# Extra products of ones with bias rows behind the last transposes of each graph-convolution layer, and one shift copy used twice

## The chip, the cores and the metric

The kernel is one launch on one core of a Trainium2 chip. The number that counts is the device time of that launch in microseconds (us); three runs of the kernel before took 3001.92 to 3007.29 us, with a median of 3004.92 us. The core has five engines that run side by side and meet through semaphores: TensorE (PE in the profile: matrix products into PSUM, with its weight loads shown as PEld), VectorE (DVE), ScalarE (ACT), GpSimd (POOL) and SyncE (SP), whose queue here only issues transfers (SPq). The profile also lists the clock that TensorE was granted, as a share of full speed; in this case it is either 1.0 or 0.5 at any moment.

## The reference

Sixteen graphs of 1024 nodes with 128 features pass through four residual layers, each followed by a normalisation over features. The change touches the second of them, three rounds of graph convolution with a batch normalisation after each:

```
def _sage(x, adj, Wr, Wx, b, mf):
    deg = jnp.clip(jnp.sum(adj, axis=-1, keepdims=True), 1.0, None)
    agg = jnp.einsum('bij,bjd->bid', adj, x) / deg
    out = agg @ Wr + x @ Wx + b
    nrm = jnp.maximum(jnp.linalg.norm(out, axis=-1, keepdims=True), NORM_EPS)
    return out / nrm * mf[..., None]

def _bn(x, g, b):
    m = jnp.mean(x, axis=(0, 1)); v = jnp.var(x, axis=(0, 1))
    return (x - m) * jax.lax.rsqrt(v + BN_EPS) * g + b

h1 = _bn(relu(_sage(x, adj_d, Wr1, Wx1, b1, mf)), g1, be1)
h2 = _bn(relu(_sage(h1, adj_d, Wr2, Wx2, b2, mf)), g2, be2)
h3 = _bn(relu(_sage(h2, adj_d, Wr3, Wx3, b3, mf)), g3, be3)
out = concatenate([h1, h2, h3], -1) @ Wl + bl
```

The mean and variance run over all graphs and nodes, so no round can use its normalised input before the round ahead of it has been finished for every graph. `adj_d` keeps few edges; nearly all nodes have only the term `x @ Wx + b`. The biases `b1`, `b2`, `b3` are all zeros in these inputs.

## The kernel before, in words

The whole is a row of phases: attention over the sixteen graphs (`phase_att`), the search for the edges that survive (`phase_pattern`), the three convolution rounds (`phase_conv`, the place of the change), and the two last layers (`phase_end`). By the timeline `phase_conv` starts its products at 1956.8 us of the span and `phase_end` its own at 2294.8 us.

`phase_conv` runs `for layer in (1, 2, 3)` and inside it a software pipeline over `SETS` = 20 sets: 16 graphs and 4 sets of "slots" (the few nodes with edges), mixed by `ORDER`. At step `i` of `range(SETS + 3)` the program writes, in this order:

- `turn(layer, i - 3)`: eight PE transposes of `u` in two halves (L1487, into `pt`), DVE statistics of each half (L1491), ACT copies of each half (L1494), and for a graph a store of the result by SP (L1501);
- `norm(i - 1)` and `scale(i - 2)`: the row norm on DVE and POOL (L1460, L1462, L1463, L1465) and `u`, the scaled relu, on DVE (L1472);
- `start(layer, i + 3)`: the load of a later input (L1370);
- `product(layer, i)`: eight fp32 products (L1417; each stands in the profile as two records, so "x16"), for slots also L1430; then `values` for a slot set (L1401), and `add_bias` (L1438): two products of `all_ones` with a bf16 row block `rows`, 128x512 each; then `squares` on ACT (L1450, L1452).

The last three steps, i = 20, 21 and 22, have no product: they hold `turn(17)`, `turn(18)` and `turn(19)`, what is left of `norm` and `scale`, and the first loads of the next layer. Then a chain of small operations makes the normalisation's factor and shift (L1547 to L1567, one of them on POOL) in `bn`. The next layer folds them in: ACT scales the weights (`w_u`, L1511), and `shifted` makes a copy of the shift over a whole tile (`shift`, L1324), multiplies it by the weights (L1326) and adds the result to the bias (L1327); `spread` turns that into bf16 rows (L1309 to L1318). At step 1, behind the first bias products, `rescale(layer - 1)` folds the same factor and shift into the last linear map: a scaled copy of `wl` (L1332), then `shifted` once more with its own copy of the same `shift`. After layer 3 `rescale(3)` does it a last time, and `extra(b0, (2,))`, eight times, adds products for the slots (L1343, L1348), whose results POOL scatters (L1581) before `phase_end` loads x (L1606) and h (L1610) by SP.

Every engine keeps the program's order: at the end of `phase_conv` and of `phase_end` the instructions of each engine are tied to each other as written (`as_traced`). Three PSUM buffers `pq` (`ps_q`, two banks each) hold products, two buffers `pt` (`ps_t`) hold transposes and small products; a buffer is used again in turn.

The lines that put the change in its place:

```
            if i < SETS:
                product(layer, i, w_u)
                ...
                for k in ((), (0, 1))[i] if i < 2 else (i,):
                    add_bias(k, bias_u if ORDER[k] < B else ROWS[layer])
                    squares(k)
            elif layer < 3:
                start(layer + 1, i - SETS)
            if layer > 1 and i == 1:
                rescale(layer - 1)
```

Of the kernel before, what the change touches and what calls it, by code (L numbers as in the profile page):

```python
# [10 lines left out]
F32 = mybir.dt.float32  # L11
# [11 lines left out]
B, N, F = 16, 1024, 128  # L23
P = 128
T = N // P
# [1246 lines left out]
def phase_conv(ctx, tc, t, c, x1_d, x1T_d, slots_d, keep, uT_d):  # L1272
# [5 lines left out]
    nc = tc.nc  # L1278
# [3 lines left out]
    ps_q = ctx.enter_context(tc.tile_pool(name="b_pq", bufs=3, space=PSUM))  # L1282
# [3 lines left out]
    SETS = B + 4  # L1286
# [8 lines left out]
    wl = cp.tile([P, 3, F], F32, name="wl")  # L1295
# [3 lines left out]
    all_ones = cp.tile([P, P], BF16, name="all_ones")  # L1299
    nc.vector.memset(all_ones, 1.0)  # L1300

    def spread(row, name):

        rest = wp.tile([P, F], F32, name="rest", bufs=1)
        sums = wp.tile([P, F], F32, name="sums", bufs=1)
        part = wp.tile([P, F], BF16, name="part", bufs=1)
        for k in range(3):
            src = row if k == 0 else rest
            nc.vector.tensor_copy(part, src)  # L1309
            nc.vector.tensor_tensor(rest, src, part, ALU.subtract)  # L1310
            if k == 0:
                nc.vector.tensor_scalar(sums, part, c.ident[:, 0:1], None, op0=ALU.mult)
            else:
                nc.vector.scalar_tensor_tensor(
                    sums, part, c.ident[:, k : k + 1], sums, op0=ALU.mult, op1=ALU.add
                )
        rows = wp.tile([P, 4, F], BF16, name=name, bufs=1)
        nc.vector.tensor_copy(rows, sums.unsqueeze(1).to_broadcast([P, 4, F]))  # L1318
        return rows.rearrange("p a f -> p (a f)")

    def shifted(to, bn, w, name):

        shift = wp.tile([P, P], F32, name="shift", bufs=1)
        nc.vector.tensor_copy(shift, bn[:, 1:2].to_broadcast([P, P]))  # L1324
        pt = ps_t.tile([P, 4, P], F32, name="pt")
        nc.tensor.matmul(pt[:, 0, :], shift, w, start=True, stop=True)  # L1326
        nc.vector.tensor_tensor(to, to, pt[:, 0, :], ALU.add)  # L1327

    def rescale(layer):

        l, bn = layer - 1, keep.bn[layer - 1]
        nc.vector.tensor_scalar(keep.wl[:, l, :], wl[:, l, :], bn[:, 0:1], None, op0=ALU.mult)  # L1332
        shifted(keep.bl, bn, wl[:, l, :], "l")

    W2, BIAS, GB = {}, {}, {}

# [22 lines left out]
    ROWS = {layer: spread(BIAS[layer], f"rows{layer}") for layer in (1, 2, 3)}  # L1359
    H, Q, R, S, U, VALUES = {}, {}, {}, {}, {}, {}  # L1360

    def slots_at(s, l):
        return uS[:, l, (s - B) * N : (s - B + 1) * N]

    def start(layer, i):

        s = ORDER[i]
        hT = H[layer, i] = wp.tile([P, N], F32, name="hT", bufs=4)
        if s < B:
            nc.sync.dma_start(hT, x1T_d[s] if layer == 1 else uT_d[layer - 2][s])  # L1370
        return hT
# [62 lines left out]
    def add_bias(i, rows):  # L1434

        pq = Q[i]
        for half in range(2):
            nc.tensor.matmul(  # L1438
                pq[:, half * 4 : half * 4 + 4, :].rearrange("p t f -> p (t f)"), all_ones,
                rows, start=False, stop=True, skip_group_check=True,  # L1440
            )
# [13 lines left out]
    def norm(i):  # L1455

        s = ORDER[i]
        square, sq = S.pop(i)
        if i % 2 == 0:
            nc.vector.tensor_reduce(sq, square, AX.X, ALU.add)  # L1460
        nrm = R[i] = small.tile([P, T], F32, name="nrm")
        nc.gpsimd.tensor_scalar(sq, sq, NORM_EPS * NORM_EPS, None, op0=ALU.max)  # L1462
        nc.gpsimd.tensor_tensor(nrm, sq, c.mhalf, ALU.pow)  # L1463
        counts = valid[:, (s - B) * HALF : (s - B + 1) * HALF] if s >= B else keep.plain[:, s, :]
        nc.gpsimd.tensor_tensor(nrm, nrm, counts, ALU.mult)  # L1465

    def scale(i):
        u = U[i] = wp.tile([P, T, F], F32, name="u", bufs=3)
        pq, nrm = Q.pop(i), R.pop(i)
        n = T if i < SETS - 1 else T // 2  # L1470
        for k in range(0, T, n):
            nc.vector.scalar_tensor_tensor(  # L1472
                u[:, k : k + n, :], pq[:, k : k + n, :], 0.0, nrm[:, k : k + n].unsqueeze(2).to_broadcast([P, n, F]),
                op0=ALU.max, op1=ALU.mult,
            )

    def turn(layer, i):
        s, u = ORDER[i], U.pop(i)
        if s >= B:
            to = slots_at(s, layer - 1)  # L1480
        else:
            to = wp.tile([P, N], F32, name="uT")
        flat = []
        for half in range(2):
            pt = ps_t.tile([P, 4, P], F32, name="pt")
            for j in range(4):
                nc.tensor.transpose(pt[:, j, :], u[:, half * 4 + j, :], c.ident)  # L1487
            flat.append(pt.rearrange("p t i -> p (t i)"))

        def stats_of(half):  # L1490
            nc.vector.bn_stats(stats[:, 2 * s + half, :], flat[half])  # L1491

        def copy(half):
            nc.scalar.copy(to[:, half * 512 : half * 512 + 512], flat[half])  # L1494

        stats_of(0)
        stats_of(1)
        copy(0)
        copy(1)
        if s < B:  # L1500
            nc.sync.dma_start(uT_d[layer - 1][s], to)  # L1501
# [4 lines left out]
    for layer in (1, 2, 3):  # L1506
        bn = keep.bn[layer - 2]
        w, w_u, bias_u = W2[layer], W2[layer][:, :F], ROWS[layer]
        if layer > 1:
            w_u = wp.tile([P, F], F32, name="w_u", bufs=1)  # L1510
            nc.scalar.activation(w_u, w[:, :F], AF.Copy, scale=bn[:, 0:1])  # L1511
            bias_u = wp.tile([P, F], F32, name="bias_u", bufs=1)
            nc.vector.tensor_copy(bias_u, BIAS[layer])
            shifted(bias_u, bn, w[:, :F], "w")
            bias_u = spread(bias_u, "rows_u")
        assert ORDER[0] < B and ORDER[1] < B
        for i in range(SETS + 3):
            if i >= 3:
                turn(layer, i - 3)
            if 2 <= i <= SETS:  # L1520
                norm(i - 1)
            if 2 <= i < SETS + 2:
                scale(i - 2)
            if i + 3 < SETS:
                start(layer, i + 3)
            if layer == 3 and i == 3:
                nc.sync.dma_start(keep.adj, t["adjT"][0].rearrange("(t p) i -> p t i", p=P))
            if i < SETS:
                product(layer, i, w_u)
                if i + 1 < SETS:  # L1530
                    values(layer, i + 1)
                if i + 2 < SETS:
                    start_slots(layer, i + 2)
# [3 lines that stand above are left out]
                if i == 1:  # L1537
                    norm(0)
            elif layer < 3:
                start(layer + 1, i - SETS)  # L1540
            if layer > 1 and i == 1:
                rescale(layer - 1)
            if layer == 3 and 4 <= i < 4 + HALF:
                extra(2 * (i - 4), (0, 1))

        mv = small.tile([P, 2], F32, name="mv")
        nc.vector.bn_aggr(mv, stats.rearrange("p a b -> p (a b)"))  # L1547
        gb = GB[layer]
        more = SETS / B
        mean = small.tile([P, 2], F32, name="mean")  # L1550

        nc.vector.tensor_scalar(mean[:, 0:1], mv[:, 0:1], more, None, op0=ALU.mult)
        nc.vector.scalar_tensor_tensor(
            mean[:, 1:2], mv[:, 0:1], mv[:, 0:1], mv[:, 1:2], op0=ALU.mult, op1=ALU.add
        )
        sc = small.tile([P, 2], F32, name="sc")
        nc.vector.tensor_scalar(
            sc[:, 0:1], mean[:, 0:1], mean[:, 0:1], BN_EPS, op0=ALU.mult, op1=ALU.subtract
        )
        nc.vector.scalar_tensor_tensor(  # L1560
            sc[:, 0:1], mean[:, 1:2], more, sc[:, 0:1], op0=ALU.mult, op1=ALU.subtract
        )
        nc.gpsimd.tensor_tensor(sc[:, 1:2], sc[:, 0:1], c.mhalf[:, 0:1], ALU.pow)
        bn = keep.bn[layer - 1]
        nc.vector.tensor_tensor(bn[:, 0:1], sc[:, 1:2], gb[:, 0:1], ALU.mult)
        nc.vector.tensor_tensor(sc[:, 0:1], mean[:, 0:1], bn[:, 0:1], ALU.mult)
        nc.vector.tensor_tensor(bn[:, 1:2], gb[:, 1:2], sc[:, 0:1], ALU.subtract)  # L1567
    rescale(3)
    as_traced(tc, first)

# [973 lines left out]
```

## Time and profile before

| | |
|---|---|
| median of three runs | 3004.92 us |
| the profiled execution, its own time | 2989.07 us |
| its span, first to last instruction | 2987.1 us |
| mean granted TensorE clock | 0.947 |

The span in parts, with busy time of each engine, the granted clock (PEclk) and the share of the transfer engines. The rows are: layer 1 of the convolution, layer 2, layer 3, the passage to `phase_end`, and `phase_end`.

```profile
1956.50:2058.00 101.50, 86.18 (x680) 77.23 (x680) 63.52 (x83) 64.76 (x240) 42.57 (x61) 0.94 0.49 168
2058.00:2160.70 102.70, 85.17 (x652) 76.15 (x652) 66.50 (x95) 65.18 (x236) 42.57 (x61) 0.92 0.47 164
2160.70:2277.80 117.10, 99.09 (x780) 90.19 (x780) 71.95 (x103) 65.07 (x234) 42.55 (x61) 0.94 0.47 171
2277.80:2294.70 16.90, 10.79 (x66) 10.51 (x66) 5.82 (x11) 0.00 (x0) 9.00 (x9) 0.70 0.35 112
2294.70:2987.00 692.30, 645.58 (x5634) 635.18 (x5634) 469.64 (x1829) 265.67 (x576) 204.85 (x232) 0.98 0.42 152
```

The columns after the length are PE, PEld, DVE, ACT and POOL in us, then clock, transfers and GB/s. In the three layers PE is the busiest engine, at 83 to 85 us of each 100, and its clock is below full there.

### The profile page before, as it was taken

To read this page: it belongs to the slowest core of one execution; us is meant where nothing else is said; L and a number is where in the kernel's file an instruction comes from. 1 tells how busy PE (TensorE), PEld (TensorE's weight loads), DVE (VectorE), ACT (ScalarE), POOL (GpSimd) and SP (SyncE) were. 2 spreads that over 40 slices of the span, in tenths; PEclk is the share of its full clock that TensorE was granted. 3 is DMA by queue.
4 is the path that set the end of the run, shared out by engine and by line. 5 is a ranking of instruction groups with operands and counts; after the bars stand their busy time and mean duration, and the time that the engine had idled before them with its cause. 6 is when DMAs were issued, how large, how long until landed. Compare 5 with 4: busy or idle time off the path is not lost. (4 is left out here: it accounts for less than half of the span.)

```text
span 2987.1 us, 71058 instructions
## 1 busy us (share of the span) xinstructions
PE 2680.9 (90%) x25724; PEld 2405.8 (81%) x25724; DVE 2252.3 (75%) x8656; ACT 1841.4 (62%) x5689; POOL 1260.1 (42%) x1305
## 2 busy tenths in 40 slices
PE   5999999999999999999997898577896999999997
PEld 3888888888888888888887887367786999999996
DVE  5798888988898888988884568756655677677674
ACT  3888888788887888888883233255653433443333
POOL 3655455644555554654322433244433233333321
PEclk8999999999999999999997777788997999999999
DMA  5324332333224332332214542054555254445540
GB/s 158 93 79 112 89 89 67 101 103 84 78 78 114 87 89 72 96 106 81 69 51 154 181 150 65 21 169 152 180 190 207 106 186 172 150 146 183 186 156 17
DMA packets 179961, 348.62 MB, mean 117 GB/s; under 512 B 14148, under 2 KB 89942, under 8 KB 179472
## 3 DMA queue, kind: packets, MB, share of 16 engines
q1 hardware_dynamic: 173584, 328.15, 34.5%
q0 software_dynamic: 4864, 11.63, 1.3%
q10 hardware_dynamic: 1152, 4.19, 0.5%
q8 instruction: 206, 3.38, 0.5%
q14 instruction: 155, 1.27, 0.1%
HBM read 257.87 MB, written 87.03 MB: 115 GB/s over the span
## 5 line engine op out<-in xcount | busy, mean ns | idle before, releaser
L583 ACT ACTIVATE hg<-pg,hg 128x128 f32<-128x128 f32 x1600 | 510.2, 365 | 28.7
L316 POOL TENSOR_SCALAR arena<-ld 104x1024 f16<-104x1024 f32 (+1 forms) x150 | 424.1, 2827 | 238.1 <-DMA ld<-in_adjT 238.0
L554 PE MATMUL pg<-parts,oh 104*128 104x384 f32 (+1 forms) x1760 | 520.7, 377 | 0.9 <-ACT hg L583 0.7
L592 PE MATMUL pa<-hg,we 128*104 128x129 f32 (+1 forms) x3520 | 516.5, 270 | 0.3 <-DVE we L539 0.3
L571 DVE SCALAR_TENSOR_TENSOR junk<-pg,w_a 128x128 bf16<-128x128 f32 x1600 | 398.9, 284 | 98.0 <-PE pg L559 96.0
L592 PEld LDWEIGHTS pa<-hg,we 128*104 128x104 f32 x3520 | 464.7, 171 | 9.5 <-DVE we L539 0.5
L559 PE MATMUL pg<-parts,oh 104*128 104x384 f32 (+1 forms) x1760 | 437.9, 330 | 0.0
L423 POOL TENSOR_TENSOR g<-k_next,off 105x512 f16<-105x512 f16 (+1 forms) x240 | 240.4, 1020 | 315.7 <-PE pw L464 291.9
L559 PEld LDWEIGHTS pg<-parts,oh 104*128 104x128 f32 x1760 | 313.5, 190 | 0.1
L554 PEld LDWEIGHTS pg<-parts,oh 104*128 104x128 f32 x1760 | 276.1, 192 | 27.4 <-issue 13.9
L581 ACT ACTIVATE hg<-sc 128x2 f32<-128x2 f32 (+1 forms) x880 | 190.0, 216 | 156.9 <-DVE junk L571 152.4
L1647 POOL TENSOR_TENSOR rstd<-ve,mhalf 128x4 f32<-128x4 f32 x96 | 98.0, 1021 | 443.3 <-DVE ve L1646 443.3
L1685 ACT COPY xT<-pt 128x512 f32<-128x512 f32 x64 | 37.5, 586 | 375.8 <-PE pt L1684 343.2
L539 DVE TENSOR_TENSOR we<-k_id,ids 128x832 f32<-128x832 f16 (+1 forms) x240 | 255.0, 1062 | 0.0
L494 ACT CAST oh<-oh_b 104x1024 fp32r<-104x1024 bf16 (+1 forms) x240 | 235.2, 980 | 2.5 <-DVE oh_b L488 2.5
L343 PE MATMUL pw<-w_all,xT 128*104 128x512 f32 x320 | 171.4, 617 | 14.9 <-DMA xT<-in_xTp 11.6
L488 DVE TENSOR_TENSOR oh_b<-pw,k_slot_edge 104x512 bf16<-104x512 f32 (+1 forms) x240 | 154.0, 642 | 15.7 <-PE pw L480 15.2
L364 DVE TENSOR_TENSOR parts<-pw,parts 104x384 fp32r<-104x384 f32 x160 | 88.4, 552 | 86.9 <-ACT own L360 86.0
L1491 DVE BATCH_NORM_STATS2 stats<-pt 128x6 f32<-128x512 f32 x120 | 79.5, 692 | 70.4 <-PE pt L1487 69.2
L571 DVE DVE_READ_ACCUMULATOR junk<-pg,w_a 128x1 f32 x1600 | 131.9, 82 | 0.0
L473 ACT CAST oh_b<-pw 104x512 bf16<-104x512 f32 (+1 forms) x240 | 131.0, 546 | 0.4
L456 DVE SCALAR_TENSOR_TENSOR one_way<-qs,arena 104x1040 bf16<-104x1040 f16 (+9 forms) x160 | 125.9, 787 | 2.2 <-ACT qs L449 2.2
(366 smaller groups left out, 6468.0 us busy)
## 6 DMA issues: line engine op xcount, KB each, us to landing
ld<-in_adjT SPq DMA_DIRECT2D x135, 416.0 KB
keep_adj<-in_adjT SPq DMA_DIRECT2D x8, 4096.0 KB
adj<-in_adjT SPq DMA_DIRECT2D x8, 4096.0 KB
mask_d<-arena SPq DMA_DIRECT2D x144, 208.0 KB
hT_d<-uT SPq DMA_DIRECT2D x48, 512.0 KB
h<-hT_d SPq DMA_DIRECT2D x48, 512.0 KB
arena<-mask_d SPq DMA_DIRECT2D x11, 2048.0 KB
hT<-hT_d SPq DMA_DIRECT2D x32, 512.0 KB
```

Of the source, the lines that this page charges most:

```text
L316: engine.tensor_scalar(mt[:n, s, :N], ld[:n], 0.0, None, op0=ALU.is_gt)
L343: nc.tensor.matmul(pw[:W], d.xT[:, s * W : (s + 1) * W], w_all, start=True, stop=False, skip_group_check=True)
L423: nc.gpsimd.tensor_tensor(v.g[:E, n0 : n0 + m, :], k_next[:E].unsqueeze(1).to_broadcast([E, m, C]), v.off[:, n0 : n0 + m].unsqueeze(2).to_ ...
L488: nc.vector.tensor_tensor(v.o[:W, n0 : n0 + m, 1, :], pw[:W, : m * C].rearrange("p (n c) -> p n c", c=C), k_slot_edge[:W].unsqueeze(1).to_ ...
L494: nc.scalar.copy(v.ends[:W, n0 : n0 + m], v.o[:W, n0 : n0 + m])
L539: nc.vector.tensor_tensor(we[:, :n, :], k_id.unsqueeze(1).to_broadcast([P, n, W]), V[b * BANDS + r].ids[:, 2 * lo : 2 * hi].unsqueeze(2).t ...
L554: nc.tensor.matmul(flat[:, first : 3 * F], own, d.parts[i][:W, p, first:], start=p == 0, stop=False, skip_group_check=True,)
L559: nc.tensor.matmul(pg[:, 1::step, :], other, reversed_parts(d.parts[j][:W, p, :], step), start=False, stop=p == 1, skip_group_check=True,)
L571: nc.vector.scalar_tensor_tensor(junk, pg[:, 1 + e, :], 0.0, w_a2, op0=ALU.max, op1=ALU.mult, accum_out=d.sc[:, at + e : at + e + 1],)
L581: nc.scalar.activation(hg[:, :ways, F], d.sc[:, at : at + ways], AF.Exp)
L583: nc.scalar.activation(hg[:, e, :F], pg[:, 3 - 3 * e, :], AF.Copy, scale=hg[:, e, F : F + 1])
L592: nc.tensor.matmul(PA[bank][:W, at : at + part.stop - part.start], we[:, 2 * (u - lo) + e, :], hg[:, e, part], start=False, stop=True, ski ...
```

## The change

`shifted` is split. `shift_of(bn)` makes the copy of the shift; `shifted(to, shift, w)` takes it ready made. In layers 2 and 3 the copy made for the bias is used for `rescale(layer - 1)` too, so one DVE copy (L1324) goes in each; in `rescale(3)` the copy is made ahead of the scaled `wl` and not behind it. `fill(n)` is new: it takes a `pq` buffer and issues n products of `all_ones` with `ROWS[1]`, the bf16 rows of layer 1's bias, each overwriting what is in one of the buffer's two banks; nothing reads them. It is called in steps 20, 21 and 22 of each layer behind `turn`, with n = 8, 6 and 15.

```
-    def shifted(to, bn, w, name):
+    def shift_of(bn):
 
         shift = wp.tile([P, P], F32, name="shift", bufs=1)
         nc.vector.tensor_copy(shift, bn[:, 1:2].to_broadcast([P, P]))
+        return shift
+
+    def shifted(to, shift, w):
+
         pt = ps_t.tile([P, 4, P], F32, name="pt")
         nc.tensor.matmul(pt[:, 0, :], shift, w, start=True, stop=True)
         nc.vector.tensor_tensor(to, to, pt[:, 0, :], ALU.add)
 
-    def rescale(layer):
+    FILL = (8, 6, 15)
+
+    def fill(n):
+
+        pq = ps_q.tile([P, T, F], F32, name="pq")
+        for k in range(n):
+            nc.tensor.matmul(
+                pq[:, k % 2 * 4 : k % 2 * 4 + 4, :].rearrange("p t f -> p (t f)"), all_ones, ROWS[1],
+                start=True, stop=True,
+            )
+
+    def rescale(layer, shift=None):
 
         l, bn = layer - 1, keep.bn[layer - 1]
+        if layer == 3:
+            shift = shift_of(bn)
         nc.vector.tensor_scalar(keep.wl[:, l, :], wl[:, l, :], bn[:, 0:1], None, op0=ALU.mult)
-        shifted(keep.bl, bn, wl[:, l, :], "l")
+        shifted(keep.bl, shift, wl[:, l, :])
...
-            shifted(bias_u, bn, w[:, :F], "w")
+            shift = shift_of(bn)
+            shifted(bias_u, shift, w[:, :F])
...
             if i >= 3:
                 turn(layer, i - 3)
+            if i >= SETS:
+                fill(FILL[i - SETS])
...
             if layer > 1 and i == 1:
-                rescale(layer - 1)
+                rescale(layer - 1, shift)
```

On PE this adds 29 products (and as many weight loads) to each layer, in program order between the transposes of `turn(17)`, `turn(18)`, `turn(19)` and the first product of what follows. On DVE it removes two copies and moves one. ACT, POOL and SP issue the same instructions in the same order.

## The prediction

> **What bounds the kernel now.** I read the page's 40 slices first (PEclk falls to 0.7 and 0.8 in the convolution layers and 0.7 in the phase before), then windows of TensorE around the end of layer 1, then the timeline there, then the waits.
>
> The windows; columns are the stretch, its length, PE busy (records), granted clock, transfer share, GB/s:
>
> ```profile
> 2041.62:2045.04 3.42, 2.57 (x22) 1.00 0.60 240
> 2045.04:2048.45 3.41, 1.06 (x8) 1.00 0.65 221
> 2048.45:2051.86 3.41, 1.94 (x8) 0.50 0.00 0
> 2051.86:2055.28 3.42, 1.94 (x8) 0.50 0.79 264
> 2055.28:2058.69 3.41, 0.56 (x3) 0.50 0.89 300
> 2058.69:2062.10 3.41, 3.41 (x18) 0.50 0.15 55
> 2062.10:2065.52 3.42, 3.42 (x32) 1.00 0.60 169
> 2065.52:2068.93 3.41, 1.18 (x7) 1.00 0.42 141
> 2068.93:2072.34 3.41, 3.22 (x15) 0.50 0.00 0
> ```
>
> With a grid of 3.41 us the clock is 1.00 or 0.50 in every row and never between: it changes only on the grid, one row late. Full clock follows a row that was all busy; half clock follows a row with 1.06 or 1.18 us of work.
>
> The PE timeline of the same place (start, duration, line, records, idle before and what ended it):
>
> ```profile
> 2045.27 1.06 PE L1487 MATMUL pt<-ident,u 128*128 128x128 f32 x8 [1.07 <-DVE u L1472]
> 2048.50 1.94 PE L1487 MATMUL pt<-ident,u 128*128 128x128 f32 x8 [2.17 <-DVE u L1472]
> 2051.91 1.94 PE L1487 MATMUL pt<-ident,u 128*128 128x128 f32 x8 [1.47 <-ACT uT L1494]
> 2058.13 0.77 PE L1326 MATMUL pt<-w,shift 128*128 128x128 f32 x2 [4.28 <-DVE shift L1324]
> 2058.68 5.37 PE L1417 MATMUL pq<-w_u,hT 128*128 128x128 f32 x32
> 2063.89 1.95 PE L1401 MATMUL pt<-w,hT 128*128 128x128 f32 x16
> 2065.68 1.03 PE L1438 MATMUL pq<-rows_u,all_ones 128*128 128x512 bf16 x4
> 2069.12 0.77 PE L1326 MATMUL pt<-wl,shift 128*128 128x128 f32 x2 [2.41 <-DVE shift L1324]
> 2072.74 1.95 PE L1430 MATMUL pq<-v,slots_w 128*128 128x128 f32 x16
> 2074.95 1.04 PE L1487 MATMUL pt<-ident,u 128*128 128x128 f32 x8
> ```
>
> The three runs of transposes stand alone with PE idle between; the last two take 1.94 us, twice the first. The 32 records behind them take 5.2 us where full clock takes 3.6. Then PE, with its next product ready, waits 2.41 us for a small DVE copy, and the product behind it is slow again. Over the three layers the wait view has that copy as PE's second worst releaser inside the layers:
>
> ```profile
> PE pt L1487 <- DVE u L1472: 23.7, 20, 2.2
> PE pt L1326 <- DVE shift L1324: 17.7, 5, 4.3
> ```
>
> Elsewhere in a layer PE is busy about 19 of 20 us, so what PE gains at these ends moves all that follows.
>
> **What the skill says.** "TensorE: Matmul & The Clock Gate", Part 1, has the two states, half and full, set by how busy PE was in a free-running window of 3413 ns. The trace agrees (grid 3.41 us, above). The page has no threshold; I take it from this trace. In the convolution layers the rows that ended in half clock held 1.06, 1.18 and 1.34 us of PE work, the poorest that kept full clock 2.07 us (1969.94 to 1973.35) and 2.21 (2263.49 to 2266.90); so it lies between 1.34 and 2.07 of 3.41. Part 4 says that transposes don't count as busy in the same way. The trace speaks against leaving them out: without its 0.9 us of transposes the row with 2.07 would be below the rows that dropped. Part 2 says that matmuls stay in program order and only weight loads are pulled ahead: a fill that isn't done delays the transposes behind it. No page says whether products of zeros count as busy, and `ROWS[1]` is zeros here; Part 1 only says that the monitor watches busy-ness.
>
> **The change part by part**, against the profiled execution (2989.07 us, span 2987.1).
>
> A fill product is the bias product's form, and costs about 0.217 us in a row ((1.03 - 0.379)/3, from the four at 2065.68 and the single duration of 0.379), twice that, 0.43, at half clock.
>
> *Where the fills stand.* In layer 1 the first run ends at 2046.3; 8 fills, 1.7 us, end at 2048.1, and the next run isn't ready until 2048.5. Its end is 2049.6; 6 fills, 1.3 us, end at 2050.9; the last run becomes ready 2.70 us after the one before it (measured with full clock in layer 3, below), at 2051.2. It ends at 2052.3, and 15 fills, 3.3 us, end at 2055.5, when the shift product isn't due until 2056.7. So all are hidden behind DVE's `u`, ACT's copies and the chain of the normalisation, with 0.3 to 1.2 us to spare. Every 3.41 us stretch now has at least 2.1 us of PE work, mostly over 2.5. So the clock stays full. If the cover were gone, 29 x 0.217 = 6.3 us a layer would be added. The buffers that fills take were read by `scale` before the transposes ahead of them could start, so no wait on another engine is added; the second fill has a wait on PE's own earlier work.
>
> *A, the last transposes.* The twin is layer 3, where the last but one run still had full clock:
>
> ```profile
> 2268.95 1.06 PE L1487 MATMUL pt<-ident,u 128*128 128x128 f32 x8 [2.17 <-DVE u L1472]
> 2271.65 1.94 PE L1487 MATMUL pt<-ident,u 128*128 128x128 f32 x8 [1.64 <-ACT uT L1494]
> ```
>
> From this run to the next is 2.70 us, against 3.41 (2048.50 to 2051.91) and 3.42 in layers 1 and 2: -0.71 each. The last run to the statistics' sum L1547 takes 2.71 us at half clock; at full, 0.66 to DVE's first statistics and 1.29 for both, with 0.06 to the next: 2.01. So -0.70 in each layer. The normalisation's chain behind it (3.5 us) stays.
>
> *B, the layer's first products.* Shift product to first product 0.55, at full clock about 0.30: -0.25. The 32 records at full clock take 2 x 1.79 = 3.58 (start to start, as at 2063.89 to 2065.68), against 5.21 in layer 2 and 5.05 in layer 3: -1.63 and -1.47. The bias rows (DVE, ready 4 us after the shift product) are needed 5.7 us after it, so they don't take over.
>
> *C, the shift copy.* Layer 1 has no rescale, so it is the twin: from `values` at 1962.72 to the first transposes at 1971.28 is 8.56 us, PE there waiting 1.74 for `u`. Layer 2 takes 11.06 (2063.89 to 2074.95), layer 3 10.99. With the copy ready PE goes on at once, and the first `u` (ACT square, DVE sum, POOL, DVE) is late next: -2.50 and -2.43. This holds whatever the fills do. The step after it, 4.38 us in layer 1 and 4.33 in layer 2, is the same in both, so the gain isn't given back there.
>
> *D, the passage to phase_end.* A's second part, -0.70. The copy ahead of `wl`: -0.20. Shift product and the wait for `wl` in place of it: -0.25. The first `extra` takes 1.79 at half clock, 0.90 at full: -0.89. Sum 2.04, taken at DVE's first sum (2280.42) and so at POOL's first scatter (2281.40). From there POOL issues one each 1.28 us whatever PE does; SP's load of x is let go at 2288.86 when the fifth lands, so the rest of the extras' gain (they end some 3.5 us earlier) brings nothing, and x, h and `phase_end` move by 2.04. The new wait of that load, on the scaled `wl`, is long past by then.
>
> Sum: 2 x (0.71 + 0.70) + 2 x 0.25 + 3.10 + 4.93 + 2.04 = 13.4 us; profiled execution 2975.7. The timed runs' median is 15.85 us above the profiled time; nothing in the views says why, so I let the difference stand: 3004.92 - 13.4 = 2991.5.
>
> Unknown costs, both ends. Where the grid falls differs from run to run: in this execution the clock rose 3.1 and 3.4 us after the layers' first products, about the earliest that a whole busy window allows, but fell before the second run of transposes, which is early; -3 to +2 us, I take 0. `phase_end` starts at half clock and its start moves against the grid: +-1.5, I take 0. Extra instruction traffic: 87 more products and loads, 0 to 1, I take 0.
>
> **Rivals.**
> 1. The clock is held through the transposes but lost before the next layer's products, because the gap behind the 15 fills (1.2 us by my sum) is longer. For it: that gap is the longest of the three. Against: even with it a window holds 2.1 us. B and D's last part go: 13.4 - 3.6 - 1.1 = 8.7, so 2996.2.
> 2. The reused copy frees nothing, since the shift product then waits for its `pt` buffer from ACT. Against: ACT's copies of `v` end at 2066.46, just where the bias products end. C goes: 8.5, 2996.4. With 1 as well: 3.8, 3001.1.
> 3. Slower: products of zeros don't count as busy, so the clock falls as before and the fills run at 0.43. Layer 1: transposes end 2050.44, 6 fills to 2053.0, 1.1 late; end 2055.0, 15 fills to 2061.5 against 2059.2: 2.2 more. The same in layer 2; layer 3 3.0: +9.6, less C and the 0.2, is +4.5: 3009.4. It decides at the window 2045 to 2048, if that ends in half clock. Against: nothing names the data. For: the profile has no window where zeros alone decide.
>
> **How the numbers follow.** Forecast 0.79, the first rival 0.07, the second 0.04, both 0.03, the third 0.07. Predicted is 2991.5. The grid's place and the start of `phase_end` give 2986 to 2996 for it; up to 2999 the first two rivals are in, which leaves out about 0.1 above. A difference of 0.2%, 6 us, is about what a measurement of this kernel can tell from none. Faster by more: forecast and single rivals, less a little for scatter, 0.86; within: both together, half of the third and that little, 0.10; slower 0.04.
>
> **What would show it.** Right: no half-clock row between 1970 and 2285; three runs of transposes of about 1.06 us in each layer; `values` to first transposes 8.6 us in layers 2 and 3; the copies' 2.41 us waits gone; layer 2 about 97 us for its 102.7; the first scatter 2 us sooner against the first statistics' sum. Wrong: fills of 0.43 us spacing, transposes waiting behind fills, or PE idle for x and h longer by what the layers gained.

## The result, and the profile after

The changed kernel takes 2989.36 us (median of 7 runs, 2983.48 to 2993.34) against 3004.47 for the kernel before (7 runs of the same session, 2997.60 to 3009.45): 15.1 us less, ratio 0.9948, 95% interval 0.9934 to 0.9963. The forecast was 2991.5, with a range of 2986 to 2996, and faster by more than 0.2%.

Its profiled execution took 2983.48 us, with a span of 2981.2 us where the kernel before had 2987.1. That is only 5.9 us, so the span alone proves little. The views show where the rest is. First the windows by part of the span, in the columns of the table shown of before (PE, PEld, DVE, ACT, POOL, clock, transfers, GB/s); the rows are layer 1, layer 2, layer 3, the passage and `phase_end`:

```profile
1963.00:2063.60 100.60, 91.57 (x709) 79.26 (x709) 63.63 (x84) 64.81 (x240) 42.66 (x61) 0.98 0.47 167
2063.60:2160.45 96.85, 86.36 (x681) 74.04 (x681) 66.03 (x94) 65.20 (x236) 42.55 (x61) 1.00 0.49 175
2160.45:2272.55 112.10, 101.40 (x809) 89.01 (x809) 71.50 (x102) 65.12 (x234) 42.53 (x61) 1.00 0.48 178
2272.55:2289.20 16.65, 8.06 (x66) 7.67 (x66) 6.00 (x12) 0.00 (x0) 8.95 (x9) 0.87 0.36 112
2289.20:2981.10 691.90, 645.44 (x5634) 635.04 (x5634) 469.51 (x1829) 265.76 (x576) 205.20 (x232) 0.98 0.42 152
```

Layers 2 and 3 have a clock of 1.00 throughout, for 0.92 and 0.94; layer 2 is 96.85 us long for 102.70, layer 3 112.10 for 117.10. Layer 1 has 0.98 because it starts at half clock. The passage gained almost nothing, which was not expected (below). Layer 1 also starts later, at 1963.1 for 1956.8: the search for the edges ahead of it, whose code is the same, took 385.2 us for 374.3 in this one execution (from the last `pg<-parts,oh` product to the last `pc<-q_node,oh`, read from the timeline). In the other two profiles of the changed kernel layer 1 started at 1957.2 and 1957.9.

The end of layer 1, windows of PE on the 3.41 us grid (length, PE busy, clock, transfers, GB/s):

```profile
2052.76:2056.18 3.42, 2.98 (x20) 1.00 0.42 153
2056.18:2059.59 3.41, 3.07 (x20) 1.00 0.22 78
2059.59:2063.00 3.41, 3.09 (x15) 1.00 0.98 356
2063.00:2066.42 3.42, 2.70 (x24) 1.00 0.54 186
```

The rows of before at this place held 0.56 to 1.94 us, most of them at 0.50 in the clock column; each now holds 2.70 or more, and the clock stays at 1.00.

The PE timeline of the same place (start, duration, line, tiles, records, idle before and what ended it):

```profile
2052.29 1.06 PE L1504 MATMUL pt<-ident,u 128*128 128x128 f32 x8 [1.07 <-DVE u L1489]
2053.19 1.89 PE L1339 MATMUL pq<-rows,all_ones 128*128 128x512 bf16 x8
2055.52 1.07 PE L1504 MATMUL pt<-ident,u 128*128 128x128 f32 x8 [0.44 <-DVE u L1489]
2056.42 1.46 PE L1339 MATMUL pq<-rows,all_ones 128*128 128x512 bf16 x6
2058.22 1.23 PE L1504 MATMUL pt<-ident,u 128*128 128x128 f32 x8 [0.34 <-ACT uT L1511]
2059.28 3.40 PE L1339 MATMUL pq<-rows,all_ones 128*128 128x512 bf16 x15
2063.72 0.46 PE L1330 MATMUL pt<-w,shift 128*128 128x128 f32 x2 [1.04 <-DVE shift L1324]
2064.01 3.74 PE L1434 MATMUL pq<-w_u,hT 128*128 128x128 f32 x32
2067.59 1.95 PE L1418 MATMUL pt<-w,hT 128*128 128x128 f32 x16
...
2070.24 0.39 PE L1330 MATMUL pt<-wl,shift 128*128 128x128 f32 x2
```

The added products (L1339) fill three stretches that were idle, and the instructions behind them are still released by what released them before: DVE's `u`, ACT's `uT`, the shift. What is left of the idle time, 0.44, 0.34 and 1.04 us, is the margin; the prediction had put it at 0.3 to 1.2. The transposes take 1.06 to 1.23 us, for 1.94. The 32 records of the next layer's first products take 3.74 us, for 5.37. In the last line the rescale's product starts without a wait, where there were 2.41 us.

The line of the shift in the view of waits, PE alone, from layer 1 to the end of layer 3 (us in total, times, longest):

```profile
PE pt L1330 <- DVE shift L1324: 3.1, 3, 1.0
```

The wait for the shift falls from 17.7 us in five times to 3.1 in three: two are gone, and the other three now begin after the added products. For these three the shorter wait is no gain in itself, since PE has only been given something to do in it.

### The profile page after: what moved, and what is told of

It reads as the page before. It is cut to its first block, busy times and chain, and to the rows that moved or that the text cites. A ratio compares the mean times of both kernels' runs of the same rounds, so it can differ in the third digit from the quotient of the medians.

```text
span 2981.2 us, 71230 instructions
## 1 busy us (share of the span) xinstructions
PE 2695.8 (90%) x25811; PEld 2407.9 (81%) x25811; DVE 2246.4 (75%) x8654; ACT 1845.1 (62%) x5689; POOL 1261.2 (42%) x1305
## 5 line engine op out<-in xcount | busy, mean ns | idle before, releaser
L554 PEld LDWEIGHTS pg<-parts,oh 104*128 104x128 f32 x1760 | 276.5, 192 | 27.6 <-issue 15.1
```

The lines of the kernel that those rows point to most:

```text
L554: nc.tensor.matmul(flat[:, first : 3 * F], own, d.parts[i][:W, p, first:], start=p == 0, stop=False, skip_group_check=True,)
```

## The experiments

The span mixes the change with parts that scatter, so the experiments are read on stretches of the timeline. The main one runs from the first `values` product of layer 1 (L1418) to the first product of `phase_end` (L1685), 332.05 us before. For before it is known from one profiled execution only. Line numbers below are those of the changed kernel.

| kernel | n of `fill` | stretch, us | median, us | ratio to before, 95% interval |
|---|---|---|---|---|
| before | none | 332.05 | | |
| after | 8, 6, 15 | 319.62 | 2989.36 | 0.9948, 0.9934 to 0.9963 |
| e1, copy alone | none | 326.95 | 2986.36 | 0.9964, 0.9950 to 0.9977 |
| e2, products alone | 8, 6, 15 | 323.47 | 2984.14 | 0.9965, 0.9945 to 0.9984 |
| e3, after again | 8, 6, 15 | 318.51 | 2981.50 | 0.9952, 0.9937 to 0.9966 |
| e4, half of them | 4, 3, 7 | 323.02 | 2986.14 | 0.9966, 0.9953 to 0.9979 |
| e5, twice of them | 16, 12, 30 | 329.28 | 2987.65 | 0.9987, 0.9976 to 0.9998 |
| e6, transposes instead | 8, 6, 15 pairs | 318.34 | 2976.87 | 0.9935, 0.9918 to 0.9951 |
| e7, last only | 0, 0, 15 | 322.87 | 2985.65 | 0.9968, 0.9946 to 0.9989 |
| e8, first two only | 8, 6, 0 | 324.58 | 2985.35 | 0.9963, 0.9950 to 0.9976 |
| e9, after a third time | 8, 6, 15 | 318.34 | 2981.66 | 0.9961, 0.9949 to 0.9973 |
| e10, more places | 8, 6, 15 | 318.22 | 2969.39 | 0.9923, 0.9910 to 0.9936 |

Medians of different sessions are not to be compared: the kernel before had 2996.67 beside e1 to e4, 2992.17 beside e5 to e8 and 2993.17 beside e9 and e10. The ratios are. Most intervals of the partial kernels overlap the full change's; the stretch, whose parts up to the first scatter repeat from one kernel to the next within 0.04 us where the work and the clock are the same, is what tells them apart. Ratio and stretch do not agree everywhere: e1's ratio stands for 10.8 us less than before (7 to 15), where 5 was expected and its stretch shows 5.1, and e6's for 19 (15 to 25), where its stretch shows 13.7. Why these two are faster than their stretch is not shown.

**The two halves alone.** e1 leaves the call of `fill` out:

```
-            if i >= SETS:
-                fill(FILL[i - SETS])
```

> The change without its fills: the shift copy is made once and used twice, and nothing stands behind the last transposes. Theory (two separate gains: the clock by the fills, PE's wait by the copy): only part C and the 0.2 us of part D come, 2 x 2.5 + 0.2 = 5 us below the kernel before, about 2999.4 against 3004.5; the last two runs of transposes of a layer at half clock (1.94 us) in most layers, values to first transposes 8.6 us in layers 2 and 3 where before took 11.0. Rival 1 (all the gain is the clock's): within 1 us of before. Rival 2 (the copy brings it all, the fills nothing): about 2989.4.

e2 keeps the products and gives `rescale` its own copy of the shift again, behind the scaled `wl`:

```
-        if layer == 3:
-            shift = shift_of(bn)
         nc.vector.tensor_scalar(keep.wl[:, l, :], wl[:, l, :], bn[:, 0:1], None, op0=ALU.mult)
+        shift = shift_of(bn)
```

> The fills of 8, 6 and 15 with the shift copy made twice as before. Theory: parts A, B and D without 0.2, 13.4 - 5.1 = 8.3 us below before, about 2996.2; all transposes of the ends near 1.06 us, the first 32 product records of layers 2 and 3 in 3.6 us, PE's wait of 2.4 us for the second copy still there and values to first transposes near 11. Rival 1 (all the gain is the clock's): about 2989.4. Rival 2 (the copy brings it all): within 1 us of before.

The changed kernel was profiled once more beside them:

> The changed kernel once more, for its own scatter and for its passage to phase_end. Theory: near 2989.4; from the last but two run of transposes of layer 3 to the first product of phase_end 27.0 us (29.07 less 2.04). The profiled execution had 28.06, with SP's load of x let go 1.3 us after the fifth scatter had landed, when a late PE signal came. Rival (the late signal belongs to the changed kernel): again about 28.

e1 shortens the stretch by 5.10 us, e2 by 8.58, both by 13.54 in e3: the parts add up to 13.68. e3's passage, from the last but two run of transposes of layer 3 to the first product of `phase_end`, takes 27.01 us, as expected, where after had 28.06. `values` to the first transposes of the layer is 8.52 and 8.51 us in e1, as in the changed kernel, and 11.15 and 11.16 in e2, about as in the kernel before. PE's timeline of e1 at the end of layer 1:

```profile
2049.45 1.78 PE L1504 MATMUL pt<-ident,u 128*128 128x128 f32 x8 [2.17 <-DVE u L1489]
2052.70 1.94 PE L1504 MATMUL pt<-ident,u 128*128 128x128 f32 x8 [1.47 <-ACT uT L1511]
2058.91 0.77 PE L1330 MATMUL pt<-w,shift 128*128 128x128 f32 x2 [4.27 <-DVE shift L1324]
2059.47 5.56 PE L1434 MATMUL pq<-w_u,hT 128*128 128x128 f32 x32
...
2067.52 0.39 PE L1330 MATMUL pt<-wl,shift 128*128 128x128 f32 x2
```

The copy's wait is gone, and the half clock is still there. Its cost moves with the place of the grid: against before, the last two runs lie 0.16 us closer together at the end of layer 1 and 0.68 further apart in layer 3, and from the last shift's product to `phase_end` it is 0.45 less. That these shifts nearly cancel, so that e1 shows almost exactly the copy's 5.0 us, is luck. In e2 it is the other way:

```profile
2057.34 3.74 PE L1433 MATMUL pq<-w_u,hT 128*128 128x128 f32 x32
...
2066.14 0.46 PE L1330 MATMUL pt<-wl,shift 128*128 128x128 f32 x2 [2.41 <-DVE shift L1324]
2066.44 2.85 PE L1433 MATMUL pq<-w,hT 128*128 128x128 f32 x16
```

The next layer's first products are full, but the 2.41 us wait is still there, and behind it the clock is lost for one row of the grid: 2.85 us for the 1.95 of full clock. So each part brings its own gain whether the other is there or not.

**How many are needed.** e4 has `FILL = (4, 3, 7)`.

> Fills of 4, 3 and 7 in place of 8, 6 and 15, the copy used twice. Theory (a 3.41 us window must hold about 1.4 to 2.0 us of PE work): between the transposes enough is left, but after 7 products PE is idle for about 3 us, and most windows there hold too little: the transposes stay at about 1.06 us, the next layer's first products are at half clock again; B and 1.1 us of D lost, 13.4 - 4.7 = 8.7 below before, about 2995.8. Rival (any work in the gaps holds the clock): about 2989.4. Rival 2 (only gap-free work holds it): all ends at half clock, near 3000.

PE's timeline of e4:

```profile
2050.93 1.67 PE L1339 MATMUL pq<-rows,all_ones 128*128 128x512 bf16 x7
2055.37 0.57 PE L1330 MATMUL pt<-w,shift 128*128 128x128 f32 x2 [2.76 <-DVE shift L1324]
2055.74 5.29 PE L1434 MATMUL pq<-w_u,hT 128*128 128x128 f32 x32
```

The stretch is 323.02 us. The last transposes keep 1.06 and 1.22 us, but the 7 products leave 2.76 us of idle time ahead of the next layer, and its first products run at half clock (5.29 us for the 3.74).

e5 doubles them, `FILL = (16, 12, 30)`; this is the price of products that outlast their cover.

> n doubled, 16, 12 and 30: what the cover of the fills is worth. Theory (products stay in program order, so a fill that isn't done delays what stands behind it): the first idle stretch has 0.44 us left over and the added 8 products take 1.74, so 1.3 us late; the second has 0.34 and gets 1.30, so about 1.0 late, at most 1.3; the third has 1.04 and gets 3.26, so 2.2 late. About 4.5 us a layer, 13 in all: from the first values of layer 1 to the first product of phase_end about 332 us instead of 318.5 to 319.6, and the time is back near the one before, 3003. The clock stays full in the layers. Rival (PE's idle time swallows them, or the chain of the normalisation doesn't wait for PE): under 322 us and no change against after.

PE's timeline of e5 at the end of layer 1:

```profile
2044.21 3.62 PE L1339 MATMUL pq<-rows,all_ones 128*128 128x512 bf16 x16
2047.67 1.04 PE L1504 MATMUL pt<-ident,u 128*128 128x128 f32 x8
2048.54 2.75 PE L1339 MATMUL pq<-rows,all_ones 128*128 128x512 bf16 x12
2051.13 1.04 PE L1504 MATMUL pt<-ident,u 128*128 128x128 f32 x8
2052.22 6.42 PE L1339 MATMUL pq<-rows,all_ones 128*128 128x512 bf16 x29
2058.48 0.39 PE L1330 MATMUL pt<-w,shift 128*128 128x128 f32 x2
```

No line has an idle time in front of it any more: the transposes stand behind the products that nobody reads (one of the last 30 has no record). From run to run it is 1.13 and 0.76 us later than in the changed kernel, and the shift's product 1.85 us. The stretch is 329.28, about 10.4 us more than with half as many (mean of after, e3 and e9: 318.8); 13 was expected, as the three delays had been put 0.2 to 0.35 us too high. The ratio agrees, 0.9987: nearly all of the gain is gone. Nothing swallows the products; what made them free was the idle time.

**Which of them.** e7 keeps only the last group, e8 only the first two (n of 0 issues nothing).

> Only the 15 products behind the last run are left, n = 0, 0 and 15. Theory: the last transposes of each layer run at half clock as before (3.4 and 2.7 us in layers 1 and 2, 2.7 and 2.7 in layer 3), the 15 start at half clock, 0.43 us each, until one whole busy window has passed, so they end 0.5 to 2.1 us behind the point where the shift product was ready, and the next layer's first products then run full (-1.6). Net of the two -1.1 to +0.5 a layer; with the copy's -4.9 the stretch from the first values of layer 1 to phase_end is 324 to 328 us, for 332 before and 319 after. Rival (15 alone hold the clock up, the first two groups are not needed): 320 to 322 us and full clock.

> Only the products behind the last two runs but one are left, n = 8, 6 and 0. Theory: the last transposes keep full clock (2.7 and 2.0 us), but the 4.4 us without work behind them cost the clock, so the next layer's first products run at half, shift product to values 5.3 to 5.8 us as before and not 3.9. Against after +1.6 to +1.9 in layers 2 and 3 and +1.1 before the first scatter: 323 to 325 us from the first values of layer 1 to phase_end. Rival (the gap is too short to cost the clock, wherever it falls on the grid): shift product to values 3.9 us, and 319 us.

PE's timeline of e7:

```profile
2052.90 1.94 PE L1504 MATMUL pt<-ident,u 128*128 128x128 f32 x8 [1.63 <-ACT uT L1511]
2054.63 5.31 PE L1339 MATMUL pq<-rows,all_ones 128*128 128x512 bf16 x15
2059.78 0.38 PE L1330 MATMUL pt<-w,shift 128*128 128x128 f32 x2
2060.00 3.74 PE L1434 MATMUL pq<-w_u,hT 128*128 128x128 f32 x32
```

and of e8:

```profile
2049.47 1.23 PE L1504 MATMUL pt<-ident,u 128*128 128x128 f32 x8 [0.34 <-ACT uT L1511]
2054.96 0.77 PE L1330 MATMUL pt<-w,shift 128*128 128x128 f32 x2 [4.26 <-DVE shift L1324]
2055.52 6.21 PE L1434 MATMUL pq<-w_u,hT 128*128 128x128 f32 x32
```

In e7 the clock was lost before the last transposes, and the 15 products take 5.31 us for 3.40, which at 0.217 us more for each slow one makes about nine slow: the shift's product waits for them, 0.7 us late, and the first products behind it are full. In e8 the transposes are full and the first products slow (6.21 us). Stretches of 322.87 and 324.58 us, for about 318.8 with all three groups: the first two together keep the transposes at full clock, the last keeps the next layer's products there, and each of these is needed. Whether the first two are both needed was not tried. e7's is 1.1 us below the range expected: in layer 1 its last run but one still had full clock, by the place of the grid, so that 0.7 us of what should have been lost was kept, and in layer 3 the shift's product was only 0.2 us late, where at least 0.5 was expected. e8's stretch is in its range, but from the shift's product to `values` it takes 6.61 and 6.31 us, above the 5.3 to 5.8 expected: how long the half clock lasts there changes with the grid.

**Do transposes count?** e6 replaces each product by two transposes of the identity, the same PE time:

```
-            nc.tensor.matmul(
-                pq[:, k % 2 * 4 : k % 2 * 4 + 4, :].rearrange("p t f -> p (t f)"), all_ones, ROWS[1],
-                start=True, stop=True,
-            )
+            for j in (0, 1):
+                nc.tensor.transpose(pq[:, k % 2 * 4 + j, :], c.ident, c.ident)
```

> Each fill product is replaced by two transposes of the identity, 128x128 fp32, of the same PE time (2 x 0.112 us for 0.217). Theory (transposes count as busy, as the window with 2.07 us of which 0.9 were transposes suggested): full clock from layer 1 to the end of layer 3 and the same segments as after, 318 to 320 us from the first values of layer 1 to phase_end. Rival (they don't count, or count less): the clock falls behind the layers' ends as before, the transposes then take twice as long and delay what stands behind them: layer ends of 3.4 and 2.7 us and more, 329 to 337 us.

PE's timeline of e6:

```profile
2051.74 3.44 PE L1340 MATMUL pq<-ident 128*128 128x128 f32 x30
2056.18 0.46 PE L1330 MATMUL pt<-w,shift 128*128 128x128 f32 x2 [1.00 <-DVE shift L1324]
2056.48 3.74 PE L1432 MATMUL pq<-w_u,hT 128*128 128x128 f32 x32
```

From 2044.75 to 2056.18 PE has nothing but transposes, which covers two whole windows of the grid (2046.06 to 2052.88, with 2.99 and 3.09 us of work), and the products behind them are full. Every part up to the first scatter is within 0.02 us of e3's. The ratio, 0.9935, is lower than those of the changed kernel, but its interval overlaps theirs; no stretch shows a reason.

**The same at other places.** e9 is the changed kernel for a third time, beside e10, which puts such products ahead of layer 1 and around the starts and the last graph of `phase_end`. `keep.idle` is a bf16 tile of zeros. The first `fill` is that of `phase_conv`, the others are a new one of `phase_end`; `products_1`, whose own lines are left out here, calls what it is given behind each of its first two products:

```
     for i in range(3):
         start(1, i)
+    fill(15)
...
+    def fill(n):
+        for _ in range(n):
+            nc.tensor.matmul(
+                pf.rearrange("p t f -> p (t f)"), keep.idle[:, :P], keep.idle, start=True, stop=True
+            )
+
     bias_1(0)
+    fill(28)
     for half in range(2):
-        products_1(0, half, range(4))
+        products_1(0, half, range(4), fill if half == 0 else None)
+    fill(8)
...
-    for half in range(2):
-        turn(0, half)
+    turn(0, 0)
+    fill(14)
+    turn(0, 1)
...
             products_1(b + 1, 1, range(2))
+        else:
+            pf = ps_p.tile([P, 4, F], F32, name="pp")
+            fill(13)
         turn(b, 1)
         for half in range(2):
             values_3(b, half)
+        if not more:
+            fill(4)
```

> The changed kernel once more, beside the next one on the same chip. From the first values of layer 1 to the first product of phase_end 318 to 320 us, as in both of its profiles so far; ratio to before 0.994 to 0.997.

> The changed kernel with the same means at other places where PE is idle for 2 to 8 us and the clock falls: 15 products ahead of layer 1's first, and zero products in phase_end, 28 ahead of its first, 3 behind each of its first two, 8 before the first transposes, 14 between the two runs of transposes of the first graph, 13 and 4 at the same places of the last graph. Theory: full clock there too. Layer 1's first products to its first values 3.9 to 5 us for 5.9 to 6.6; phase_end 2 to 4 us shorter at its start, and another 3 to 4 where its last graph had lost the clock (phase_end 695 in some profiles, 692 in others): 688 to 690 us. Together 5 to 8 us less than the changed kernel. Rival (the fills delay the first products or the x load, since their buffer is free only when DVE has read the last extras): first scatter to the first product of phase_end over 13.6 us and no gain.

e9's stretch is 318.34 and its ratio 0.9961. e10 takes 2969.39 us beside its 2981.66, and the intervals of the two ratios don't touch. Layer 1's first product to its first `values` is 4.55 us for 5.87, `phase_end` 689.2 for 695.9: 8.0 us less, at the upper end of what was expected. The two profiled spans differ by 10.7; the rest lies ahead of layer 1's first product, most of it in the search for the edges, whose code is the same. PE's timeline of e10 at the start of `phase_end`:

```profile
2270.85 5.99 PE L1801 MATMUL pp<-keep_idle 128*128 128x512 bf16 x27
2278.01 0.46 PE L1686 MATMUL pp<-keep_wl,h 128*128 128x128 f32 x2 [1.17 <-DMA h<-hT_d]
```

The first product still waits for the load of h (1.17 us), so the products (27 of the 28 have a record) cost nothing, and it takes 0.46 us, where it took 0.76 at half clock in the changed kernel. The first scatter to the first product is 12.9 us, not over 13.6, so the rival, that they would hold up the load, is out. From layer 1's first product to the last graph's neighbour products no half clock is left.

## Why the prediction was right

The steps of the sum, beside the three profiles of the changed kernel (after, e3, e9), from starts in the timeline:

| step | before, us | after, e3, e9 | difference | forecast |
|---|---|---|---|---|
| A: last but one run to last, layers 1 and 2, each | 3.41 | 2.70, 2.70, 2.70 | -0.71 | -0.71 |
| A: last run to the statistics' sum, each layer | 2.71 | 2.00, 2.00, 2.00 | -0.71 | -0.70 |
| B: shift's product to `values`, layer 2 | 5.76 | 3.87, 3.87, 3.87 | -1.89 | -1.88 |
| B: the same, layer 3 | 5.61 | 3.87, 3.87, 3.87 | -1.74 | -1.72 |
| C: `values` to first transposes, layer 2 | 11.06 | 8.52, 8.52, 8.52 | -2.54 | -2.50 |
| C: the same, layer 3 | 10.99 | 8.52, 8.51, 8.51 | -2.47 | -2.43 |
| D: layer 3's sum to the first scatter | 7.05 | 5.86, 5.86, 5.86 | -1.19 | -1.34 |
| D: first scatter to `phase_end`'s first product | 13.38 | 14.29, 13.23, 13.01 | +0.91, -0.15, -0.37 | 0 |
| sum | | | -12.4, -13.5, -13.7 | -13.4 |

(The sum counts the first row twice and the second three times.) A and B were shown to come from the added products and C from the copy, by e1 and e2, each without the other. That products of zeros count as busy, which no view of before could decide, is shown by the grid's row 2059.59 to 2063.00 above, which held nothing else and kept its clock; so the third rival, the slower one, is out. The first rival, a clock lost in the gap behind the 15, did not occur: 1.04 us were left, while the gaps that lost it in e4 and e8 were 2.76 and 4.26 us. The second, that the reused copy frees nothing, is refuted by e1.

The match to hundredths in A and B is better than the forecast could know. Its before side came from the same profile as the table's, and the half clock costs something else in each execution: from the shift's product to `values` before has 5.76 and 5.61 us, and the kernels that lose the clock there (e1, e4, e8) have 5.29 to 6.61. The full-clock side, 3.87 in both layers of all three profiles of the changed kernel, is what was really forecast. The place of the grid, put at -3 to +2 us and taken as 0, was read off one execution. One reading was too high: away from its ends a layer has PE busy for 17.5 to 19.4 of 20 us, not for about 19; nothing in the sum rests on it, since C was taken from layer 1 as its twin.

D is the step that fits least. Its terms: the shift's product to DVE's first sum went from 2.51 to 1.39 us, -1.12, where 1.14 was forecast. The copy ahead of `wl`, put at -0.20, brought 0.07 (sum to shift's product 3.56 to 3.49): behind the instruction that makes the shift, the copy started after 0.27 us in before, with the scaled `wl` in between, and after 0.19 now that it is next. Putting it first thus moved it by 0.08 us and not by the 0.20 between the two starts. The passage itself was longer by 0.9 us in the profile of after, and not in e3 and e9. In that profile DVE's last sum of the extras starts at 2283.65 after an idle time of 2.19 us, for which the view names only "remote", and SP's load of x is issued at 2283.68. What held it up is open; it came once in the three profiles.

The median fell by 15.1 us (the interval is about 11 to 20) and the steps give 12.4 to 13.7; the ratios of e3 and e9 correspond to 14 and 12 us. The forecast took over the 15.85 us between the profiled execution of before and its median, unexplained. That the time itself, 2991.5, came within 2.1 us is in part luck: in the other sessions the kernel before had medians of 2992 to 2997 us. What makes up the 15.85 was not settled, but the profiles show scatter of that kind outside the change: the search for the edges differs by 11 us between two of them, and `phase_end` takes 691.9 us in after, 695.6 in e3 and 695.9 in e9. The last difference has a cause, shown in the last section.

## What to carry to other kernels

Where the bounding TensorE has gaps of 1 to 5 us, price the slow work behind each gap as well as the gap: here 29 unread products a layer were worth about 8.5 us in three layers, because they fit in idle time and end before their successor is ready. They were wide products, of 512 columns; narrow ones were not tried, and may not do (last section). Measure that cover first, from the timeline, and stop short of it: half as many gave up half of that, twice as many all of it and 2 us more (329.28 for e1's 326.95). And look for a small operand made twice, if the second one is what a busy engine waits for.

## What was unexpected of the hardware

**Neither limit is a full window.** The prediction put the limit that holds the clock between 1.34 and 2.07 us of 3.41. The runs narrow it. In the last graph of `phase_end` PE has a gap of about 3.3 us, and the grid decides how it is cut. Windows of e9:

```profile
2933.51:2936.92 3.41, 1.42 (x13) 1.00 0.00 0
2936.92:2940.34 3.42, 2.15 (x10) 0.50 0.00 0
```

and of the kernel before:

```profile
2946.16:2949.57 3.41, 1.43 (x13) 1.00 0.00 0
2949.57:2952.99 3.42, 2.14 (x19) 1.00 0.00 0
```

With 1.42 us of work the clock was lost, with 1.43 it was kept. All eleven profiles with that gap agree: the row of the gap held 0.4 to 1.42 us in the seven that lost the clock (e1, e3, e4, e6, e7, e8, e9) and 1.43 to 1.6 in the four that kept it (before, after, e2, e5). It explains most of the scatter of that phase: `phase_end` takes 691.9 to 692.3 us where the clock was kept, 694.6 and 694.7 where it was lost for one row (e1, e6), and 695.6 to 696.5 where for three.

Upwards no whole window is needed either: at half clock a row of e6 with 2.76 us (2936.94 to 2940.35) was followed by full clock. One of e1 with 2.79 us (2291.99 to 2295.40) was not, so the busy time of the view does not order the cases near this limit.

Nor is the busy time of the view what decides in general. In the search for the edges, in the kernel before, one row was busy throughout and the clock was lost behind it:

```profile
1567.17:1570.58 3.41, 3.41 (x140) 1.00 0.02 5
1570.58:1574.00 3.42, 2.92 (x110) 0.50 0.04 10
```

Nearly all of its 140 products are one column wide (128x1 in the timeline), where the products of the layers have 128 or 512 columns. The limits above hold for the products of the layers and of `phase_end`, from which they were read. That the width counts is the nearest reading; no run here tests it.

The Trainium skill, "TensorE: Matmul & The Clock Gate", Part 1, speaks of one idle window to lose the clock and one busy window to gain it; by these rows, for such products, a window that is two fifths busy can count as idle, and one that is four fifths busy can be enough.

**Transposes and zeros count as busy.** The same page's Part 4 says that transposes don't count in the same way. In e6 they alone held the clock for whole windows, as well as products did. The measurement decides, for fp32 transposes of this form; whether they use the mode that the page speaks of can't be read from the trace. Products of ones with zeros held it in the row of 2059.59 to 2063.00 above.
